# A recurrent head stage with 64-token pair products, its outputs and k^T v in the pair products' PSUM banks, and a planner that counts shape changes

## The chip, the cores and the metric

The kernel runs on one core of one Trainium2 chip. The core has a matrix engine (TensorE, PE in the profile, with PEld for its weight loads), a vector engine (VectorE, DVE), an activation engine (ScalarE, ACT), a general engine (GpSimd, POOL) and a queue engine for transfers (SyncE, SP). The metric is the device time of one execution in microseconds. Before the change it is 3298.43 us, the median of three runs (3298.05 to 3305.83).

## The reference

Input is x of 2 x 4096 x 256 in fp32. A layer norm modulated by a conditioning vector is followed by two RWKV layers (time mix and channel mix), a residual, a second modulated norm and a feed-forward net whose operands are rounded to FP4 in blocks of 16. The change touches the recurrence in the time mix, four heads of 64 channels each:

```python
def step(state, inp):
    rt, kt, vt, wt = inp
    kv = kt[..., :, None] * vt[..., None, :]
    out = jnp.einsum('bhk,bhkv->bhv', rt, state + u[None, :, :, None] * kv)
    return (state * wt[..., None] + kv, out)
```

So the output at a token is r times the decayed sum of all earlier k^T v, with the weight u instead of a decay for the token itself. Each head's output is then scaled to unit variance over its 64 channels.

## The kernel before

**Tiles and streams.** Work goes in tiles of 256 tokens (`TT`), two chunks of 128 tokens (`C`) each. The 256 channels are two groups of 128 (`J`), and each holds two heads of 64 (`HS`). There are 16 tiles per batch element, two batch elements and two layers, so 64 calls of `wkv`. Four generators (`first_layer` and `second_layer`, for each batch element) make the layers' work, a fifth (`ffns`) the feed-forward net of the 32 finished tiles, and two more prepare weights and conditioning.

**The planner.** Every operation is recorded (`record`, `weight` gives its cost) and issued in an order that `Plan.run` chooses: the operation that can start first by the planner's own clock, and among those of its engine that can start within 40 ns (`SOON`) the most urgent, then the oldest. Successive matmuls of a generator make one operation. The clock is not measured, so an operation's place is fixed when the kernel is built. `need` finds dependencies by comparing partitions and columns of a tile. All instructions are issued from one line, line 248 in the profile (`give_out`), so the profile is read by tile names. Evacuated PSUM results live in 36 working tiles (`slot`). Five PSUM banks are shared and handed out at issue (`bank`, `close`).

**The head stage (`wkv`).** A lock (`head_lock`) lets one head stage at a time use `pa`, two PSUM banks, one for each head of a channel group. A stage is more urgent than other work (`RUSH`) while it holds the lock. It runs seven levels. At level l, products of k and r give the scores of token pairs whose positions first differ in bit l, while the decays between them are multiplied into r and k on DVE from level to level (`pair_view`), and the decay products are halved in number. Levels 0 to 4 multiply 32 tokens by 32: per level 2 chunks, 2 groups, 4 blocks and 2 heads, 32 products of 64 channels. Level 5 makes 16 such products off the diagonal, level 6 eight of 64 by 64 tokens. Levels 0 to 3 have a place each in `pa`. After level 3 four masked copies (`copy_predicated`, a mask for each level) collect them in `diag`; level 4 is collected after level 6, when two more plain copies move levels 5 and 6 into `attn`. Four copies then spread `diag` along the diagonal of `attn`.

**Outputs and state.** For each chunk, r is multiplied with the state `S` (128 x 128 for a channel group, two heads, with zeros off the diagonal), the scores in `attn` with v, both into one shared bank `po`; then k^T v of the chunk goes to a bank of its own, `kv`. DVE updates the state from `kv`, ACT squares the outputs, DVE sums the squares. After the second chunk the lock is given back; a power on POOL and one multiplication on DVE scale the outputs from `po` to a working tile.

Of the kernel before, what the change touches and what calls it, by code (L numbers as in the profile page):

```python
# [10 lines left out]
I32 = mybir.dt.int32  # L11
# [20 lines left out]
LEAST = (8, 5, 3)  # L32
RUSH = 1.0
SOON = 40.0
SLOTS = 36
STAGGER = (12, 60)
SLOTS2 = 4
TINY = 24
# [51 lines left out]


class Op:
    __slots__ = ("eng", "calls", "cost", "port", "wait", "ready", "next", "end", "banks", "tiles", "age", "late")

    def __init__(self, eng, age):
        self.eng, self.age = eng, age
        self.calls, self.banks, self.tiles, self.next = [], {}, set(), []
        self.cost = self.ready = self.end = 0.0
        self.port = False
        self.wait = 0  # L100


class Plan:
# [15 lines left out]
    SEEN = {"tensor": 55.0, "gpsimd": 80.0}  # L119
    SAME = {"vector": 34.0, "scalar": 25.0, "gpsimd": 80.0}  # L120

    def after(self, o, op):
        return o.end + (self.SAME.get(o.eng, 0.0) if o.eng == op.eng else self.LAT[o.eng] + self.SEEN.get(op.eng, 35.0))

    def __init__(self, nc, banks):
        self.nc, self.banks = nc, [(0.0, b) for b in banks]
        self.probe = banks[0]
        self.seen = {}
        self.held = {}
        self.free = {e: 0.0 for e in self.ENG}  # L130
        self.lock = {"vector": 0.0, "gpsimd": 0.0}
        self.cur = None
        self.count = 0
        for e in self.ENG:
            setattr(self, e, Recorder(self, e))
# [67 lines left out]
    def record(self, eng, fn, a, k):  # L203
        st = self.cur
        outs = [k["out"]] if "out" in k else [a[0]]
        ins = list(a[0 if "out" in k else 1:]) + [v for n, v in k.items() if n != "out"]
        ins = [v for v in ins if isinstance(v, (bass.AP, Later))]
        cost, port = weight(eng, fn, outs[0], ins)
        op = st.last if eng == "tensor" else None
        if op is None or op.next is None:  # L210
            self.count += 1
            op = Op(eng, self.count)
            op.late = st.late
            st.queue.append(op)
        st.last = op if eng == "tensor" else None
        op.calls.append((getattr(getattr(self.nc, eng), fn), a, k))
        op.cost += cost
        op.port = op.port or port
        for v in ins:
            if not is_dram(v):  # L220
                self.need(op, v, False)
        for v in outs:
            if not is_dram(v):
                self.need(op, v, True)

    def start(self, op, st):
# [7 lines left out]
            t = max(t, self.lock["gpsimd" if op.eng == "vector" else "vector"] - 100.0)  # L234
        return t

    def give_out(self, op, t):
        for b in op.banks:
            if b.real is None:
# [6 lines left out]

        for fn, a, k in op.calls:
            fn(*[real(v) for v in a], **{n: real(v) for n, v in k.items()})  # L248
        op.end = t + op.cost
        self.free[op.eng] = t + (60.0 if op.eng == "sync" else op.cost - self.LAP.get(op.eng, 0.0))  # L250
        if op.port:
            self.lock[op.eng] = op.end
        for b in op.banks:
# [62 lines left out]
        return lambda *a, **k: self.plan.record(self.eng, fn, a, k)  # L316


def is_dram(v):
    return isinstance(v, bass.AP) and v.name.endswith("_dram")  # L320


def weight(eng, fn, out, ins):
# [4 lines left out]

    n = max(v.free_size() for v in [out] + ins)
    if eng == "tensor":  # L330
        if fn == "transpose":
            return 110.0, False
        n = out.free_size()
        if n <= 32:
            return 19.0, False
        pair = (n == 64 and out.shape[0] == 64) or (ins[0].shape[0] <= 64 and out.shape[0] == P and n == TT)
        return (4 * n / 2.4 + 6) * (0.55 if pair else 1.0), False
    if eng == "sync":
        return 100.0, False
    wide = [v for v in ins if v.free_size() > 1]  # L340
# [17 lines left out]
def rwkv_adaln_fp4_kernel(ctx: ExitStack, tc: tile.TileContext, a: dict, out: bass.AP):  # L358
# [28 lines left out]

    masks = const.tile([P, NLEV, 32], I32, name="masks")  # L390
    with tc.tile_pool(name="mk", bufs=1) as mk:
        s_i = mk.tile([P, 32], I32, name="s_i")
        t_i = mk.tile([P, 32], I32, name="t_i")
        x_i = mk.tile([P, 32], I32, name="x_i")
        g_i = mk.tile([P, 32], I32, name="g_i")
        y_i = mk.tile([P, 32], I32, name="y_i")
        nc.gpsimd.iota(s_i, pattern=[[0, 32]], base=0, channel_multiplier=1)
        nc.gpsimd.iota(t_i, pattern=[[1, 32]], base=0, channel_multiplier=0)
        nc.vector.tensor_scalar(s_i, s_i, 31, None, ALU.bitwise_and)
# [9 lines left out]

    ps = ctx.enter_context(tc.tile_pool(name="ps", bufs=1, space=PSUM))  # L410
    pa = ps.tile([P, 2, 512], F32, name="pa")
    kv = ps.tile([P, C, J, P], F32, name="kv")
    banks = [ps.tile([P, 512], F32, name=f"bank{n}") for n in range(5)]

    wk = ctx.enter_context(tc.tile_pool(name="work", bufs=1))

# [165 lines left out]
        pl.comes(t, when)  # L582


    state = [[keep.tile([P, J, P], F32, name=f"S{i}_{b}") for b in range(B)] for i in range(L)]
    carry = [
        [[keep.tile([P, J, 1], F32, name=f"carry{i}_{b}_{m}") for m in range(2)] for b in range(B)]
        for i in range(L)
# [6 lines left out]
    diag = keep.tile([P, 2, C, J, 32], F32, name="diag")  # L595
    attn = keep.tile([P, 2, C, J, P], F32, name="attn")
    nc.gpsimd.memset(diag, 0.0)
    nc.vector.memset(kv, 0.0)
    nc.gpsimd.memset(attn, 0.0)


# [140 lines left out]
    def wkv(i, b, rk_s, dec_s, v_s):  # L742
# [20 lines left out]
        for l in range(7):  # L763
            h = 1 << l
            R, K = (r0, k0) if l == 0 else (r, k)
            wid = 64 if l == 6 else 32
            col0 = (l % 4) * C * J * 32
            cols = slice(col0, col0 + C * J * wid)
            pv = pa[:, :, cols].rearrange("p a (c j t) -> p a c j t", c=C, j=J)

            if l < NLEV:
                at0 = [(q, q) for q in (0, 32, 64, 96)]
            else:
                at0 = [(0, 32), (64, 96)] if l == 5 else [(0, 64)]
            for c in range(C):
# [21 lines left out]
            pl.vector.tensor_tensor(nt, tv[:, :, 0], tv[:, :, 1], ALU.mult)  # L797
            tot = nt

            ready = {3: range(0, 4), 6: range(4, 7)}.get(l, ())  # L800
            for m in ready:
                mw = 64 if m == 6 else 32
                c0 = (m % 4) * C * J * 32
                mc = slice(c0, c0 + C * J * mw)
                if m < NLEV:
                    pl.vector.copy_predicated(
                        diag.rearrange("p a c j t -> p a (c j) t"),
                        masks[:, m, :].unsqueeze(1).unsqueeze(1).to_broadcast([P, 2, C * J, 32]),
                        pa[:, :, mc].rearrange("p a (n t) -> p a n t", t=32),
                    )  # L810
                else:
                    for s0, t0 in [(0, 32), (64, 96)] if m == 5 else [(0, 64)]:
                        pl.scalar.copy(
                            attn[s0 : s0 + mw].rearrange("p a c j t -> p a (c j) t")[:, :, :, t0 : t0 + mw],
                            pa[s0 : s0 + mw, :, mc].rearrange("p a (n t) -> p a n t", t=mw),
                        )
            yield
        give(dec_s)
        tot = tot.rearrange("p (c j) -> p c j", c=C)
        for q in range(4):  # L820
            qs = slice(32 * q, 32 * (q + 1))
            pl.scalar.copy(
                attn[qs].rearrange("p a c j t -> p (a c j) t")[:, :, qs],
                diag[qs].rearrange("p a c j t -> p (a c j) t"),
# [8 lines left out]
        pl.close(bk)  # L833
        yield
        o_s, sq_s = take_slot(), take_slot()
        o_sb, sq = v3(o_s), v3(sq_s)
        bk, po = pl.bank()
        po = halves(po)
        n = C * H
        few = pl.take(tiny)  # L840
        rs = few[:, :n]
        for c in range(C):
            for j in range(J):
                mm(po[:, c, j * P : (j + 1) * P], r[:, c, j, :], S[:, j, :], True, False)
                for p in range(2):
                    hd = slice((2 * j + p) * HS, (2 * j + p + 1) * HS)
                    mm(po[:, c, hd], attn[:, p, c, j, :], v[:, c, hd], False, p == 1)

# [8 lines left out]
            pl.scalar.activation(sq[:, c, :], po[:, c, :], AF.Square)  # L857
# [440 lines left out]
```

## Time and profile before

| | |
|---|---|
| median of three runs | 3298.43 us |
| the profiled execution | 3307.55 us |
| its span in the profile | 3305.8 us |
| mean granted TensorE clock | 0.967 of full speed |
| DMA | 42.31 MB, mean 13 GB/s |
| pair products of 32 tokens (`pa`, 64x32) | 22528 records, mean 200 to 202 ns |
| r times S (`bank<-S,slot`) | 512 records, mean 297 ns |
| attn times v (`bank<-slot,attn`) | 1024 records, mean 264 ns |
| k^T v (`kv`) | 1024 records, mean 235 ns |
| state update on DVE | 256, mean 343 ns |
| activation table loads on ACT | 133, mean 1283 ns |

Durations come from one profiled execution. A row of a group gives its line, engine, operation, output and input names with shapes, the count, the busy time in us and the mean in ns of one, and then the idle time of the engine just before them and what ended it. In a timeline a row gives start, length, engine, group and the number of records. One fp32 matmul is two records. A matmul's record is its whole passage through the array, so records overlap, and the distance from start to start says what it costs; the shape behind the name (64*32) is the rows and columns of the array that it uses.

### The profile page before, as it was taken

Reading aid. Unit: us, or ns where it says so; the run is one execution under the profiler, and the core shown is the slowest. Engines: PE = TensorE matmul, PEld = TensorE weight load, DVE = VectorE, ACT = ScalarE, POOL = GpSimd, SP = SyncE. Lnnn points to the kernel's source line nnn. Section 1 sums busy time; section 2 is a strip of 40 time slices with the busy share of each in tenths; the row PEclk is TensorE's granted clock in tenths of the full one; section 3 lists DMA queues with packets and bytes.
Section 4 is the critical chain, followed back from the end, with each engine's and each line's share of the span. In section 5 each row is a group of like instructions: output and inputs, shape, how many; then the busy total and the mean of one; then the engine's idle time right before and its main releaser. Section 6 shows DMA issues by size and latency. Waiting matters only on the chain. (4 is left out here: it accounts for less than half of the span.)

```text
span 3305.8 us, 88142 instructions
## 1 busy us (share of the span) xinstructions
PE 3075.7 (93%) x37948; PEld 2448.4 (74%) x37948; DVE 2396.8 (73%) x6146; ACT 1628.8 (49%) x3240; POOL 938.5 (28%) x857
## 2 busy tenths in 40 slices
PE   3899999999999999999999999999999999999965
PEld 1678778777777877777887777877777877877743
DVE  3777687777777687777777777778767787866764
ACT  1455455555555555555555555455554555444321
POOL 1233223233223233323233322333322233321200
PEclk8899999999999999999999999999999999998977
DMA  4000000000000000000000000000000000000000
GB/s 126 17 16 5 11 9 14 5 8 14 8 11 5 15 8 11 8 9 11 8 15 8 11 8 5 17 5 15 4 8 15 8 15 8 5 8 8 14 4 10
DMA packets 46856, 42.31 MB, mean 13 GB/s; under 512 B 13185, under 2 KB 44930, under 8 KB 46466
## 3 DMA queue, kind: packets, MB, share of 16 engines
q1 hardware_dynamic: 36962, 31.75, 3.2%
q8 instruction: 298, 4.88, 0.6%
q10 hardware_dynamic: 9504, 4.93, 0.5%
q14 instruction: 92, 0.75, 0.1%
HBM read 28.28 MB, written 8.39 MB: 11 GB/s over the span
## 5 line engine op out<-in xcount | busy, mean ns | idle before, releaser
L248 POOL TENSOR_TENSOR slot<-slot,slot 128x512 f32<-128x512 f32 x416 | 499.5, 1214 | 1016.4 <-DVE slot L248 614.9
L248 ACT ACTIVATE slot<-bank 128x512 f32<-128x512 f32 (+1 forms) x644 | 338.9, 531 | 753.3 <-PE bank L248 714.9
L248 POOL TENSOR_TENSOR tiny<-tiny,nhalf 128x2 f32<-128x2 f32 (+1 forms) x288 | 295.0, 1028 | 1018.2 <-DVE tiny L248 960.5
L248 DVE TENSOR_TENSOR slot<-slot,slot 128x512 f32<-128x512 f32 x512 | 381.6, 747 | 121.4 <-PE pa L248 88.7
L248 PE MATMUL bank<-slot,cWk 128*128 128x256 f32 x1536 | 375.8, 391 | 14.5 <-DVE slot L248 12.3
L248 PE MATMUL bank<-cWv,slot 128*128 128x256 f32 x1536 | 345.4, 381 | 0.0
L248 PEld LDWEIGHTS pa<-slot 64*32 64x32 f32 x19456 | 226.0, 109 | 156.3 <-DVE slot L248 56.5
L248 PEld LDWEIGHTS bank<-slot,cWk 128*128 128x128 f32 x1536 | 289.4, 194 | 62.1 <-DVE slot L248 15.7
L248 PEld LDWEIGHTS bank<-cWv,slot 128*128 128x128 f32 x1536 | 289.4, 190 | 41.0 <-ACT slot L248 0.7
L248 ACT ACTIVATE slot<-bank,vec 128x256 f32<-128x256 f32 x512 | 234.4, 496 | 166.6 <-PE bank L248 159.4
L248 PE MATMUL pa<-slot 64*32 64x32 f32 x19456 | 271.6, 203 | 38.0 <-DVE slot L248 24.0
L248 DVE SCALAR_TENSOR_TENSOR slot<-bank,vec,slot 128x256 f32<-128x256 f32 x640 | 275.1, 474 | 29.5 <-PE bank L248 28.1
L248 DVE TENSOR_TENSOR slot<-slot,bank 128x512 f32<-128x512 f32 x192 | 131.3, 684 | 200.8 <-PE bank L248 173.1
L248 POOL TENSOR_TENSOR slot<-slot 128x512 f32<-128x512 f32 x128 | 143.2, 1120 | 322.8 <-ACT slot L248 253.0
L248 DVE TENSOR_TENSOR long<-long,bank 128x352 f32<-128x352 f32 x256 | 131.7, 515 | 113.9 <-ACT long L248 91.7
L248 ACT ACTIVATE slot<-slot,tiny 128x256 f32<-128x256 f32 x256 | 141.8, 593 | 135.7 <-DVE tiny L248 114.7
L248 PE MATMUL bank<-ident,slot 128*128 128x128 f32 x1152 | 181.3, 286 | 23.9 <-ACT slot L248 18.1
L248 ACT ACT_TABLE_LOAD x133 | 170.6, 1283 | 46.6 <-DMA td<-in_L_attn_td_w_dram 38.3
L248 PE MATMUL bank<-wd,long 128*128 128x256 f32 x768 | 192.3, 403 | 1.2 <-ACT long L248 1.2
L248 PE MATMUL bank<-wg,slot 128*128 128x352 f32 x512 | 180.0, 474 | 4.6 <-ACT slot L248 4.4
L248 PEld LDWEIGHTS bank<-ident,slot 128*128 128x128 f32 x1152 | 136.6, 144 | 61.7 <-ACT slot L248 24.0
L248 DVE SCALAR_TENSOR_TENSOR slot<-slot,vec,slot 128x256 f32<-128x256 f32 x384 | 177.6, 493 | 5.8 <-POOL slot L248 5.7
(112 smaller groups left out, 5837.0 us busy)
## 6 DMA issues: line engine op xcount, KB each, us to landing
slot<-in_L_attn_x_dram SPq DMA_DIRECT2D x63, 256.0 KB, 2.7
out_dram<-slot SPq DMA_DIRECT2D x32, 256.0 KB, 2.1
cWv<-in_L_attn_cWv_dram SPq DMA_DIRECT2D x1, 768.0 KB, 9.4
cWk<-in_L_attn_cWk_dram ACTq DMA_DIRECT2D x1, 768.0 KB, 8.1
slot<-in_L_wmod_dram SPq DMA_DIRECT2D x3, 256.0 KB, 7.3
slot<-in_L_wmod_dram ACTq DMA_DIRECT2D x3, 256.0 KB, 6.5
cWk<-in_L_attn_cWk_dram SPq DMA_DIRECT2D x1, 768.0 KB, 4.8
cWv<-in_L_attn_cWv_dram ACTq DMA_DIRECT2D x1, 768.0 KB, 8.4
```

Of the source, the lines that this page charges most:

```text
L248: fn(*[real(v) for v in a], **{n: real(v) for n, v in k.items()})
```

## The change

1. Levels 0 to 4 multiply 64 tokens by 64: two blocks for the two halves of a chunk, so 16 products per level. `diag` and the masks are 64 tokens wide. A level needs twice the room in `pa`, so there are two places, used in turn. Levels are collected after level 1 (0 and 1), after level 3 (2 and 3), after level 5 (4 and 5) and after level 6. Level 5 goes to `diag`, and two copies of 64 partitions spread `diag` into `attn`.
2. k^T v of both chunks is computed ahead of the outputs, into the first half of `pa`'s first bank.
3. The state holds 64 columns for a channel group instead of 128. r is multiplied with it head by head, 64 channels each, 64 rows of the array at a time: four products of 64 columns per chunk where there were two of 128.
4. The outputs go to the second half of `pa`'s two banks, a bank for each head of a group. The scaling reads them there, and the lock is given back and the urgency ends behind it.
5. `kv` has no bank of its own, and the shared banks are six. There are 35 working tiles.
6. The planner adds a cost where an engine's operation differs in form from its last one: 94 ns on TensorE for another shape, 1283 ns on ScalarE for another of Sigmoid and Exp. Costs of matmuls go by shape.

```diff
-SLOTS = 36
+SLOTS = 35
...
+    TURN = {"tensor": 94.0, "scalar": 1283.0}
...
+        f = form(eng, fn, outs[0], ins, a)
+        if f is not None:
+            if op.forms and op.forms[-1] != f:
+                op.cost += self.TURN[eng]
+            op.forms.append(f)
...
+    def turn(self, op):
+
+        return self.TURN[op.eng] if op.forms and op.forms[0] != self.form[op.eng] else 0.0
...
-        op.end = t + op.cost
-        self.free[op.eng] = t + (60.0 if op.eng == "sync" else op.cost - self.LAP.get(op.eng, 0.0))
+        op.end = t + op.cost + self.turn(op)
+        if op.forms:
+            self.form[op.eng] = op.forms[-1]
+        self.free[op.eng] = t + (60.0 if op.eng == "sync" else op.end - t - self.LAP.get(op.eng, 0.0))
...
+def form(eng, fn, out, ins, a):
+    if eng == "tensor":
+        return (ins[0].shape[0], P if fn == "transpose" else out.shape[0])
+    if eng == "scalar" and fn == "activation" and a[2] in (AF.Sigmoid, AF.Exp):
+        return a[2]
...
-        n = out.free_size()
-        if n <= 32:
-            return 19.0, False
-        pair = (n == 64 and out.shape[0] == 64) or (ins[0].shape[0] <= 64 and out.shape[0] == P and n == TT)
-        return (4 * n / 2.4 + 6) * (0.55 if pair else 1.0), False
+        if rows == P and cols == P:
+            return max(4 * n / 2.4 + 6, 195.0 if n == 64 else 265.0 if n == P else 0.0), False
+        if n <= 64:
+            return {(64, 32): 22.0, (64, 64): 66.0, (P, 64): 70.0, (64, P): 66.0}.get((rows, cols), 2 * n), False
+        return 0.55 * (4 * n / 2.4 + 6), False
...
-    kv = ps.tile([P, C, J, P], F32, name="kv")
-    banks = [ps.tile([P, 512], F32, name=f"bank{n}") for n in range(5)]
+    banks = [ps.tile([P, 512], F32, name=f"bank{n}") for n in range(6)]
...
-    state = [[keep.tile([P, J, P], F32, name=f"S{i}_{b}") for b in range(B)] for i in range(L)]
+    state = [[keep.tile([P, J, HS], F32, name=f"S{i}_{b}") for b in range(B)] for i in range(L)]
...
-            wid = 64 if l == 6 else 32
-            col0 = (l % 4) * C * J * 32
+            wid = 32 if l == 5 else 64
+            col0 = 0 if l == 6 else (l % 2) * C * J * 64
...
-                at0 = [(q, q) for q in (0, 32, 64, 96)]
+                at0 = [(0, 0), (64, 64)]
...
-            ready = {3: range(0, 4), 6: range(4, 7)}.get(l, ())
-            for m in ready:
+            for m in {1: (0, 1), 3: (2, 3), 5: (4, 5), 6: (6,)}.get(l, ()):
...
-        for q in range(4):
-            qs = slice(32 * q, 32 * (q + 1))
+        for q in range(2):
+            qs = slice(64 * q, 64 * (q + 1))
...
-        bk, po = pl.bank()
-        po = halves(po)
+        po = pa[:, :, 256:].rearrange("p a (c j v) -> p a c j v", c=C, j=J)
+        kv = pa[:, 0, :256].rearrange("p (c j v) -> p c j v", c=C, j=J)
...
-                mm(po[:, c, j * P : (j + 1) * P], r[:, c, j, :], S[:, j, :], True, False)
                 for p in range(2):
                     hd = slice((2 * j + p) * HS, (2 * j + p + 1) * HS)
-                    mm(po[:, c, hd], attn[:, p, c, j, :], v[:, c, hd], False, p == 1)
-
+                    mm(kv[p * HS : (p + 1) * HS, c, j, :], kt[:, c, hd], v[:, c, hd], True, True)
+        yield
+        for c in range(C):
+            for j in range(J):
+                for p in range(2):
+                    hp = slice(p * HS, (p + 1) * HS)
+                    mm(po[:, p, c, j, :], r[hp, c, j, :], S[hp, j, :], j == 0, False)
             for j in range(J):
                 for p in range(2):
                     hd = slice((2 * j + p) * HS, (2 * j + p + 1) * HS)
-                    mm(kv[p * HS : (p + 1) * HS, c, j, p * HS : (p + 1) * HS], kt[:, c, hd], v[:, c, hd], True, True)
+                    mm(po[:, p, c, j, :], attn[:, p, c, j, :], v[:, c, hd], False, j == J - 1)
...
-                head_lock.clear()
-                pl.cur.late = late
...
-            o_sb.rearrange("p c (h v) -> p (c h) v", v=HS), po.rearrange("p c (h v) -> p (c h) v", v=HS),
-            rs.unsqueeze(2).to_broadcast([P, n, HS]), ALU.mult,
+            o_s[:, : J * TT].rearrange("p (n a v) -> p a n v", a=2, v=HS),
+            pa[:, :, 256:].rearrange("p a (n v) -> p a n v", v=HS),
+            rs.rearrange("p (n a) -> p a n", a=2).unsqueeze(3).to_broadcast([P, 2, C * J, HS]), ALU.mult,
         )
-        pl.close(bk)
+        head_lock.clear()
+        pl.cur.late = late
```

More of the change, by code (lines that the diff above doesn't have):

```diff
@@ L92 @@
 class Op:
-    __slots__ = ("eng", "calls", "cost", "port", "wait", "ready", "next", "end", "banks", "tiles", "age", "late")
+    __slots__ = ("eng", "calls", "cost", "port", "wait", "ready", "next", "end", "banks", "tiles", "age", "late", "forms")
     def __init__(self, eng, age):
@@ L98, in __init__ @@
         self.cost = self.ready = self.end = 0.0
+        self.forms = []
         self.port = False
@@ L131, in __init__ @@
         self.lock = {"vector": 0.0, "gpsimd": 0.0}
+        self.form = {"tensor": None, "scalar": None}
         self.cur = None
@@ L330, in weight @@
     if eng == "tensor":
+        n, rows, cols = out.free_size(), ins[0].shape[0], out.shape[0]
         if fn == "transpose":
             return 110.0, False
-        n = out.free_size()
-        if n <= 32:
-            return 19.0, False
-        pair = (n == 64 and out.shape[0] == 64) or (ins[0].shape[0] <= 64 and out.shape[0] == P and n == TT)
-        return (4 * n / 2.4 + 6) * (0.55 if pair else 1.0), False
+        if rows == P and cols == P:
[3 more added lines that the diff above has]
+        return 0.55 * (4 * n / 2.4 + 6), False
     if eng == "sync":
@@ L386, in rwkv_adaln_fp4_kernel @@
     nc.gpsimd.memset(nhalf, -0.5)
-    masks = const.tile([P, NLEV, 32], I32, name="masks")
+    masks = const.tile([P, NLEV, 64], I32, name="masks")
     with tc.tile_pool(name="mk", bufs=1) as mk:
[L392 to L399, printed above, removed]
+        s_i = mk.tile([P, 64], I32, name="s_i")
+        t_i = mk.tile([P, 64], I32, name="t_i")
+        x_i = mk.tile([P, 64], I32, name="x_i")
+        g_i = mk.tile([P, 64], I32, name="g_i")
+        y_i = mk.tile([P, 64], I32, name="y_i")
+        nc.gpsimd.iota(s_i, pattern=[[0, 64]], base=0, channel_multiplier=1)
+        nc.gpsimd.iota(t_i, pattern=[[1, 64]], base=0, channel_multiplier=0)
+        nc.vector.tensor_scalar(s_i, s_i, 63, None, ALU.bitwise_and)
         nc.vector.tensor_tensor(x_i, s_i, t_i, ALU.bitwise_xor)
@@ L594, in rwkv_adaln_fp4_kernel @@
                 nc.gpsimd.memset(carry[i][b][m], 0.0)
-    diag = keep.tile([P, 2, C, J, 32], F32, name="diag")
+    diag = keep.tile([P, 2, C, J, 64], F32, name="diag")
     attn = keep.tile([P, 2, C, J, P], F32, name="attn")
     nc.gpsimd.memset(diag, 0.0)
-    nc.vector.memset(kv, 0.0)
     nc.gpsimd.memset(attn, 0.0)
@@ L798, in wkv @@
             tot = nt
-            ready = {3: range(0, 4), 6: range(4, 7)}.get(l, ())
-            for m in ready:
-                mw = 64 if m == 6 else 32
-                c0 = (m % 4) * C * J * 32
+            for m in {1: (0, 1), 3: (2, 3), 5: (4, 5), 6: (6,)}.get(l, ()):
+                mw = 32 if m == 5 else 64
+                c0 = 0 if m == 6 else (m % 2) * C * J * 64
                 mc = slice(c0, c0 + C * J * mw)
@@ L807, in wkv @@
                         diag.rearrange("p a c j t -> p a (c j) t"),
-                        masks[:, m, :].unsqueeze(1).unsqueeze(1).to_broadcast([P, 2, C * J, 32]),
-                        pa[:, :, mc].rearrange("p a (n t) -> p a n t", t=32),
-                    )
-                else:
-                    for s0, t0 in [(0, 32), (64, 96)] if m == 5 else [(0, 64)]:
+                        masks[:, m, :].unsqueeze(1).unsqueeze(1).to_broadcast([P, 2, C * J, 64]),
+                        pa[:, :, mc].rearrange("p a (n t) -> p a n t", t=64),
+                    )
+                else:
+                    dst = diag if m == 5 else attn
+                    for s0, t0 in [(0, 32), (64, 32)] if m == 5 else [(0, 64)]:
                         pl.scalar.copy(
-                            attn[s0 : s0 + mw].rearrange("p a c j t -> p a (c j) t")[:, :, :, t0 : t0 + mw],
+                            dst[s0 : s0 + mw].rearrange("p a c j t -> p a (c j) t")[:, :, :, t0 : t0 + mw],
                             pa[s0 : s0 + mw, :, mc].rearrange("p a (n t) -> p a n t", t=mw),
@@ L835, in wkv @@
         o_s, sq_s = take_slot(), take_slot()
-        o_sb, sq = v3(o_s), v3(sq_s)
-        bk, po = pl.bank()
-        po = halves(po)
+        sq = v3(sq_s)
+        po = pa[:, :, 256:].rearrange("p a (c j v) -> p a c j v", c=C, j=J)
+        kv = pa[:, 0, :256].rearrange("p (c j v) -> p c j v", c=C, j=J)
         n = C * H
@@ L856, in wkv @@
                 )
-            pl.scalar.activation(sq[:, c, :], po[:, c, :], AF.Square)
+            pl.scalar.activation(
+                sq[:, c, :].rearrange("p (j a v) -> p a j v", j=J, a=2), po[:, :, c, :, :], AF.Square
+            )
             pl.vector.tensor_reduce(
```

## The prediction

> **What bounds the kernel now.** First the busy times of the page, then the stages.
>
> ```profile
> span 3305.8 us, 88142 instructions
> PE 3075.7 (93%) x37948; PEld 2448.4 (74%) x37948; DVE 2396.8 (73%) x6146; ACT 1628.8 (49%) x3240; POOL 938.5 (28%) x857
> ```
>
> The matrix engine (PE) is the bound, the vector engine is 20 points behind. The view by windows (columns: window, length, then PE, PEld, DVE, ACT, POOL busy) says where:
>
> ```profile
> 1500.00:2000.00 500.00, 487.17 (x6046) 390.30 (x6047) 377.14 (x966) 265.09 (x524) 155.44 (x140) 1.00 0.04 11
> 3200.00:3306.00 106.00, 60.70 (x193) 42.54 (x191) 53.65 (x100) 16.71 (x31) 5.55 (x5) 0.76 0.02 8
> ```
>
> From 500 to 3000 us PE is busy 97% of the time. The last 180 us are a chain of feed-forward tiles, one output every 38 us, which the change doesn't touch. So the sum is made per head stage (one call of `wkv`, 64 in all, one every 51 us), in PE time. A busy PE hides its gaps, so I take the spacing of starts from PE's timeline (start, length, group, count; one fp32 product is two records):
>
> ```profile
> 2411.03 1.89 PE L248 MATMUL bank<-Wo,slot 128*128 128x256 f32 x8
> 2412.85 0.76 PE L248 MATMUL pa<-slot 64*32 64x32 f32 x64
> 2413.54 0.70 PE L248 MATMUL bank<-slot,w 128*128 128x256 f32 x2
> ...
> 2417.85 0.68 PE L248 MATMUL pa<-slot 64*64 64x64 f32 x16
> 2418.46 0.70 PE L248 MATMUL bank<-slot,w2b 32*128 32x256 f32 x4
> ...
> 2423.07 0.38 PE L248 MATMUL bank<-S,slot 128*128 128x128 f32 x2
> 2423.30 0.56 PE L248 MATMUL bank<-slot,attn 128*128 128x64 f32 x4
> 2423.69 0.44 PE L248 MATMUL bank<-S,slot 128*128 128x128 f32 x2
> 2423.97 0.56 PE L248 MATMUL bank<-slot,attn 128*128 128x64 f32 x4
> 2424.45 0.45 PE L248 MATMUL kv<-slot,slot 128*64 128x64 f32 x8
> 2424.83 1.99 PE L248 MATMUL bank<-Wv,slot 128*128 128x256 f32 x8
> 2426.66 0.38 PE L248 MATMUL bank<-S,slot 128*128 128x128 f32 x2
> ```
>
> To be seen: a level of 32 pair products takes 0.69 us to the next start; level 6 (8 products on two 64x64 tiles) 0.61; one chunk of outputs 1.38, its k^T v 0.38. Eight records of 128x256 are 0.216 each, 1.73, in a row of their own shape; before another shape (Wo) they take 1.82, after one (Wv) 1.83. So leaving a shape costs about 0.10 us and coming back 0.10.
>
> **The change on PE, per head stage.** *Pair levels 0 to 4*: 32 products of 64x32 become 16 of 64x64 on four tiles. No row shows four such tiles. Level 6 ran two row tiles at once (0.61 for 8), k^T v two column tiles at once (0.38 for 4 products), and the present levels eight small ones. If four run at once, 16 products take what 8 take on two, 0.61, with a stagger 0.63; if two at a time, eight more steps of 58 ns (level 6's spacing of record pairs), 1.08. Nearest are the rows that show each split alone: I take 0.63. 5 x (0.63 - 0.69) = -0.30 us; worst +1.95.
>
> *k^T v*: twice 0.38, with 0.10 in and 0.10 out each (1.16; the 0.10 in is inside the 1.38 above), becomes one group of 16 records on two tiles, level 6's 0.61, plus 0.20: 0.81.
>
> *Output products*: the 12 records of a chunk take 1.38, less 0.10 for leaving, 107 ns each, whether 128 or 64 columns stream: what binds is the loading of 128 weight columns. After the change r times S is four products of 64 rows by 128 columns on two row tiles, a shape of its own. Nearest by count is k^T v, 8 records on two tiles in 0.38; but that loads 64 columns. The Trainium skill (TensorE: Matmul & The Clock Gate, LDWEIGHTS) says that a load costs by its columns, not by its rows: 128 columns are 107 ns with 64 rows too. By it the four steps take 4 x 0.11 + 0.05 + 0.10 = 0.60; by the k^T v row 0.38. The 107 ns of the outputs decide for the rule. Then 8 attn records, 8 x 0.11 + 0.10 for re-entry = 0.98, and 0.10 before r times S: 1.68 a chunk. Both chunks with k^T v: 2 x 1.68 + 0.81 = 4.17, against 2 x (1.38 + 0.38 + 0.10) = 3.72 now. +0.45 us: two more shape changes per chunk cost more than the zero blocks.
>
> PE together: -0.30 + 0.45 = +0.15 us x 64 = **+10 us**; ends -18 (r times S at 0.38) and +150 (pairs two at a time).
>
> **DVE and ACT.** The rows by shape:
>
> ```profile
> L248 DVE COPY_PREDICATED diag<-masks,pa 128x256 f32<-128x256 int32 x320 | 139.9, 437 | 23.4 <-ACT attn L248 13.0 <-PE pa L248 7.1 <-ACT slot L248 1.3
> L248 DVE TENSOR_TENSOR long<-long,bank 128x352 f32<-128x352 f32 x256 | 131.7, 515 | 113.9 <-ACT long L248 91.7 <-PE bank L248 20.9
> L248 DVE TENSOR_TENSOR slot<-slot,bank 128x512 f32<-128x512 f32 x192 | 131.3, 684 | 200.8 <-PE bank L248 173.1 <-ACT slot L248 20.4 <-issue 6.1
> L248 ACT COPY attn<-diag 32x256 f32<-32x256 f32 x256 | 103.0, 402 | 17.9 <-DVE diag L248 14.2 <-DVE tiny L248 0.5
> L248 ACT COPY attn<-pa 64x512 f32<-64x512 f32 x64 | 36.6, 572 | 6.8 <-DVE diag L248 6.4
> ```
>
> An element costs (684 - 515) / 160 = 1.06 ns, so the masked copy of 512 columns takes 437 + 256 x 1.06 = 707 ns: 5 x 270 = +1.35 us. Four state updates lose 64 columns (TENSOR_TENSOR of 128 columns 302, of 64 241): -0.24. DVE +1.1 us, 71 us in all, busy from 73% to 75%. ACT: four copies of 402 become two of 572, -0.46. Neither binds; both lie under PE's other work, except in the head's own chain.
>
> **The chain and the shared banks.** Now levels 0 to 3 have four places and are copied together after level 3; only level 4 waits for copies. Its start follows level 3's by 5.2 us in the median, where levels 2, 3 and 5 follow by 2.6 to 3.2. After the change there are two places, and levels 2, 4 and 6 wait for copies of 0.7 us. The planner compares columns (`need`), so it lets one copy run beside the next level. The Trainium skill (PSUM — Partial Sum Buffer, PSUM bank collisions) says that two engines must be kept off one bank and 32-partition quadrant at any columns. The trace agrees: of 512 reads of the pair banks (320 masked, 192 plain) none overlaps a matmul into them. By the planner's rule a level waits for one copy; by the banks', for all that are issued before it, 0.7 us later than planned, and queued behind it in PE's order is everything else. Likewise k^T v and both outputs now lie in these two banks: state updates (DVE), squares (ACT) and the next chunk go one after the other. Cost: nothing if PE arrives late anyway, up to 4 x 0.4 = 1.6 us a stage if it doesn't. The nearest row is level 4: PE lost 3.1 us before it in 64 stages, 0.05 each. Three levels more and the chunks at twice that: 0.25 us x 64 = **+16 us**.
>
> The lock on the pair banks is held longer. From the first pair product to the last k^T v are 31 us in the mean; now the next head may start its pairs earlier, and in 22 of 64 cases did before or within 5 us of that end. After, the banks come free with the scaling, 4 us later at best (9 in the mean, but its urgency now lasts till there), and copies add 1 to 2 us: 36 to 38 us of 51. PE's gaps beyond the spacing of its shape sum to 107 us in the 1650 us inside these stretches and 23 in 850 outside (500 to 3000): 6.5% and 2.7%. Six us longer x 3.8% x 64 = +15; in part it is the above: **+12 us**; ends 0 and +90.
>
> **Planner and sixth bank.** The waits of the weight queue, same window (us, times, longest):
>
> ```profile
> PEld pa L248 <- DVE slot L248: 44.5, 95, 1.5
> PEld bank L248 <- ACT slot L248: 26.9, 50, 2.1
> PEld pa L248 <- ACT slot L248: 18.5, 43, 2.1
> ```
>
> With the smaller rows ACT releases a third of the waits for data, a third of 130 us, 43. The 133 table loads of 1.28 us aren't in today's plan and are in the new one; so are 94 ns for a PE shape, of the 0.20 that it costs. Against this, 64x64 is planned at 66 ns a product where my 0.63 gives 33. Banks: a group holds one about 2.7 us (from a projection's start to its evacuation's end), some 31 groups a stage, plus the output's 15: 2 of 5 in use on average, so a sixth is rarely the one missing. Between 0 and -65 (half of the gaps); I take a third of ACT's share, **-15 us**. One working tile fewer (35 of 36): nothing.
>
> **Sum.** 10 + 16 + 12 - 15 = +23 us. The profiled execution took 3307.55 (span 3305.8, 1.75 around it), 0.3% above the median 3298.43; on the median, **3321 us**.
>
> **Rivals.** *A better plan wins* (not slower): the place is PE's gaps behind ACT and DVE, 130 us. It decides from 38 us removed, the 23 and the 15 already counted. For it: those gaps are waits that a truer plan fills; against: inside a head they come from a chain that gets longer. At half, 65 us: 3298 + 38 - 65 = 3271. *Nothing measurable*: the terms cancel, 3298. *The pair banks become the bound*: 38 us of 51 is no limit for heads spread evenly, but their starts lie 20 to 81 us apart; where two or three streams stand at the lock, PE has one stream and the feed-forward left. At the upper end, +90: 3298 + 11 + 90 = 3399. For it: spacings under 36 us now become impossible; against: long gaps exist into which they can move. *The four tiles don't run together*: (1.08 - 0.63) x 5 x 64 = +144, 3465; against it stand both two-tile rows.
>
> **Chances.** Forecast (3309 to 3365) 0.42; better plan 0.25; nothing 0.13; banks bound 0.15; tiles 0.05. About 0.3% (10 us) is what this kernel's runs can tell from no change. Faster 0.25, same 0.13, slower 0.42 + 0.15 + 0.05 = 0.62. For 8 in 10 the range reaches half into the better plan and most of the way to the banks' case: 3245 to 3400.
>
> **What would show it.** In PE's timeline: 16 products of 64x64 with the next start 0.63 us on (1.08: tiles); r times S at 0.60 (0.38: the load rule wrong); k^T v at 0.61. The masked copy at 707 ns. PE gaps above 130 us between 500 and 3000, with "PE pa <- DVE" grown; from first pair to scaling under 40 us. Wrong if ACT-released waits fall to half, or if heads start at intervals of 40 us in an unbroken row, which is the lock. The tail alone can move it 14 us: one feed-forward tile more or less left at 3130 us (38 us, some 24 of them PE).

## The result and the profile after

The changed kernel takes 3308.68 us (median of 13 runs, 3302.11 to 3323.3) against 3298.71 us: 1.0044 of the time before, with a 95% interval of 1.0026 to 1.0063. It is slower, by 10 us between the medians and by 14 us by the ratio. Two of the 13 executions of before, of 5975 and 11991 us, lie far outside all others and don't enter the ratio. The forecast was 3321 us, its range 3245 to 3400.

The profiled execution took 3320.43 us, span 3318.3, some 12 us above the median, as that of before lay 9 above its own. The page's first lines after the change:

```profile
span 3318.3 us, 68391 instructions
PE 3066.0 (92%) x28220; PEld 2407.3 (73%) x28220; DVE 2490.9 (75%) x6145; ACT 1591.1 (48%) x3112; POOL 947.9 (29%) x857
```

PE's busy time fell by 10 us while the span grew by 12.5, so PE stood idle 22 us longer. Where, the windows show, first of before, then of after (columns: window, length, PE, PEld, DVE, ACT and POOL busy with counts, PE's granted clock, DMA share, GB/s):

```profile
500.00:3000.00 2500.00, 2433.32 (x30748) 1950.23 (x30747) 1866.61 (x4796) 1313.50 (x2602) 753.33 (x670) 0.99 0.03 10
3000.00:3306.00 306.00, 225.28 (x1632) 169.77 (x1631) 190.50 (x417) 87.24 (x170) 45.08 (x40) 0.84 0.03 9
```

```profile
500.00:3000.00 2500.00, 2392.17 (x22360) 1884.99 (x22359) 1922.36 (x4739) 1253.66 (x2444) 752.07 (x658) 0.99 0.03 9
3000.00:3318.00 318.00, 261.95 (x1825) 201.00 (x1823) 212.50 (x476) 112.23 (x216) 55.15 (x49) 0.90 0.03 9
```

In the main stretch PE is idle 108 us instead of 67; behind 3000 us it is idle 56 instead of 81. The head stages end later and the feed-forward net has caught up more by then, so the last stretch is better filled (its granted clock is 0.90 instead of 0.84): the last head stage ends at 3192 us instead of 3125, yet the kernel ends only 12.5 us later.

The products themselves are to be read from PE's timeline (start, length, group, records, and idle time ahead of it with its releaser; all instructions now come from line 262):

```profile
1519.78 0.69 PE L262 MATMUL pa<-slot 64*64 64x64 f32 x32
1520.40 0.70 PE L262 MATMUL bank<-slot,w2b 32*128 32x256 f32 x4
1521.03 0.66 PE L262 MATMUL bank<-ident,slot 128*128 128x128 f32 x4
1522.02 0.69 PE L262 MATMUL pa<-slot 64*64 64x64 f32 x32 [0.34 <-DVE slot L262]
...
1540.91 0.66 PE L262 MATMUL pa<-S,slot 64*128 64x64 f32 x8
1541.50 1.10 PE L262 MATMUL pa<-slot,attn 128*128 128x64 f32 x8
1542.54 0.69 PE L262 MATMUL pa<-slot,slot 128*64 128x64 f32 x16
1543.15 2.86 PE L262 MATMUL bank<-wd,long 128*128 128x256 f32 x12
```

A level of 16 products takes 0.62 us to the next start (0.63 was forecast, 0.69 before), r times S of a chunk 0.59 (0.60), k^T v of both chunks 0.61 (0.61). The state update and the masked copy:

```profile
L262 DVE COPY_PREDICATED diag<-masks,pa 128x512 f32<-128x512 int32 x320 | 231.1, 722 | 8.9 <-PE pa L262 7.3
L262 DVE SCALAR_TENSOR_TENSOR S<-S,slot,pa 128x64 f32<-128x64 f32 x256 | 62.6, 277 | 92.9 <-PE pa L262 54.7 <-ACT slot L262 37.5
```

And what the weight queue (PEld) waits for from 500 to 3000 us (us, times, longest): the waits of the pair products on DVE.

```profile
PEld pa L262 <- DVE slot L262: 63.0, 95, 3.2
...
PEld pa L262 <- DVE diag L262: 31.8, 36, 1.8
```

`DVE slot`, the decayed r and k, was 44.5 before; `DVE diag`, the masked copies, was 3.2. What ACT releases (`slot`, `diag`, `attn` and `long`) is 57 us before and after.

The same from PE's side: its idle time just before the pair products, over the whole span, with what ended it. Before, these are levels 1 to 5; after, levels 1 to 4 and 6:

```profile
L248 PE MATMUL pa<-slot 64*32 64x32 f32 x18432 | 226.7, 202 | 32.5 <-DVE slot L248 21.7 <-DVE diag L248 5.6 <-DVE carry L248 2.5
```

```profile
L262 PE MATMUL pa<-slot 64*64 64x64 f32 x9216 | 222.5, 225 | 61.7 <-DVE diag L262 24.4 <-DVE slot L262 20.4 <-DVE tiny L262 7.9
```

With the level that stands in a row of its own (5.5 us before, 12.0 after) that is 38.0 us before and 73.7 after.

**How gaps and work are told apart below.** I sum what lies between the starts of neighbouring PE records beyond the usual distance of the same pair of shapes; that is "gaps", over the whole span. The span less the gaps is PE's "work", shape changes and reloads included. Before: gaps 295 us, work 3011. After: gaps 293, work 3025. So by this count PE got 14 us more work, the gaps between 100 and 3000 us grew from 170 to 200 us, and those behind 3000 shrank from 110 to 78. Where the line between the two lies depends on what is called usual. A second count from the same records takes blocks of one shape against the usual length of such a block: it finds 3014 us of work before and 3015 after, gaps of 166 and 209 us between 100 and 3000 us, and 109 and 78 behind. The 44 us that the stretch up to 3000 us lost are the same in both (14 + 30, or 1 + 43); a difference of some 15 us in work is not to be relied on.

Gaps before the pair products of levels 2 to 6 are listed apart, since they can be placed: 10.5 us before, 53.9 after. This too is a count of that kind. PE's plain idle time at these places is 11 and 55 us from 500 to 3000 us, and 28 and 70 us over all 64 head stages.

### The profile page after: what moved, and what is told of

The parts are those of the page before. It is cut to its first block, busy times and chain, and to the rows that moved or that the text cites. A ratio compares the mean times of both kernels' runs of the same rounds, so it can differ in the third digit from the quotient of the medians.

```text
span 3318.3 us, 68391 instructions
## 1 busy us (share of the span) xinstructions
PE 3066.0 (92%) x28220; PEld 2407.3 (73%) x28220; DVE 2490.9 (75%) x6145; ACT 1591.1 (48%) x3112; POOL 947.9 (29%) x857
## 5 line engine op out<-in xcount | busy, mean ns | idle before, releaser
L262 POOL TENSOR_TENSOR slot<-slot,slot 128x512 f32<-128x512 f32 x416 | 511.4, 1245 | 892.9 <-DVE slot L262 535.7
L262 ACT ACTIVATE slot<-bank 128x512 f32<-128x512 f32 (+1 forms) x516 | 292.0, 567 | 568.8 <-PE bank L262 551.7
L262 PEld LDWEIGHTS pa<-slot 64*64 64x64 f32 x11264 | 203.7, 132 | 190.1 <-DVE slot L262 72.2
L262 PE MATMUL pa<-slot 64*64 64x64 f32 x11264 | 252.4, 220 | 73.7 <-DVE slot L262 31.6
L262 DVE COPY_PREDICATED diag<-masks,pa 128x512 f32<-128x512 int32 x320 | 231.1, 722 | 8.9 <-PE pa L262 7.3
L262 ACT ACT_TABLE_LOAD x133 | 170.6, 1283 | 48.9 <-DMA td<-in_L_attn_td_w_dram 38.6
```

## The experiments

The ratios are to the kernel before on the same chip. Each profile gives work and gaps.

**A plan that differs for no reason.** 36 working tiles instead of 35:

```diff
-SLOTS = 35
+SLOTS = 36
```

> The changed kernel with 36 working tiles instead of 35: a part of the change undone that should be worth nothing of itself. It shows how far a different but equivalent plan moves the time. Every theory: 3309 us, within 8 us; anything beyond is the chance of the plan, and other differences must be read against it.

Measured 3313.11 us, ratio 1.0047 (1.0029 to 1.0065): the same as the change, as expected; how far another plan can go, one such pair doesn't say. Work 3027, gaps 284; before levels 2 to 6, 45 us.

**The planner of before in the changed kernel** (no forms, no `turn`, the old costs):

```diff
...
-        op.end = t + op.cost + self.turn(op)
+        op.end = t + op.cost
...
```

> The changed kernel with the planner of before (no form changes, old costs); nothing else differs. My theory (the plan is worth 15 us): 3324. Rival (the new plan does harm, since it plans a 64x64 product at 66 ns where 33 are measured): 3295. If within 8 us of 3309, the planner's part is worth nothing.

Measured 3308.11 us, 1.0041 (1.0026 to 1.0056). In this pair of plans the planner's part is worth nothing measurable: neither the 15 us that I counted for it nor harm from a price of 66 ns for a product that costs half. It does move waits: what ACT releases for the weight queue is 75 us with the planner of before and 57 with the new one, while `DVE slot` and `DVE diag` together are 69 with the old and 95 with the new.

**Five shared banks in the changed kernel:**

```diff
-    banks = [ps.tile([P, 512], F32, name=f"bank{n}") for n in range(6)]
+    banks = [ps.tile([P, 512], F32, name=f"bank{n}") for n in range(5)]
```

> The changed kernel with five shared banks, the sixth left unused. My theory (2 of 5 banks in use on average): 3309 to 3315. Rival (the sixth bank is what pays for the rest): 3330 or more.

Measured 3353.3 us, 1.0182 (1.0151 to 1.0212), 45 us above the change, as the rival expected. In the profiles it is 28 us, all of it gaps (327; work 3019). That speaks against my count, by which a sixth bank is rarely missed. How much of the 45 us is the bank's own, and how much a plan that happens to be worse, one run doesn't say (see the halved interpolations below).

**The wide state, outputs in one shape.** The state with its zero blocks again, outputs in the second pair bank; 34 working tiles; the core of the edit:

```diff
-        po = pa[:, :, 256:].rearrange("p a (c j v) -> p a c j v", c=C, j=J)
+        po = pa[:, 1, :].rearrange("p (c n) -> p c n", c=C)
...
-                    mm(po[:, p, c, j, :], r[hp, c, j, :], S[hp, j, :], j == 0, False)
+                mm(po[:, c, j * P : (j + 1) * P], r[:, c, j, :], S[:, j, :], True, False)
...
+                    pl.vector.scalar_tensor_tensor(
+                        S[hp, j, hp], S[hp, j, hp], tot[hp, c, j : j + 1], kv[hp, c, j, :], ALU.mult, ALU.add
+                    )
```

> The changed kernel with the state 128 columns wide again, zero blocks and all: r times S and attn times v go through the array in one shape, as before, into the second pair bank alone, and k^T v stays alone in the first; 34 working tiles. The state update takes 8 instructions of 64 partitions a stage instead of 4. My theory: a chunk's outputs cost 1.38 us of PE again instead of 1.68, -0.6 us x 64 = -38 us, 3271; some of it is lost to the longer state update (0.55 us a chunk), so 3271 to 3285. Rival (the lock and the pair banks set the time, shape changes of PE don't): 3300 to 3312, with PE's gaps grown by what the products gained.

Measured 3413.22 us, 1.035 (1.033 to 1.0369). The work fell to 2979, by 46 us against the change (27 in the second count): the price of the split outputs, 38 us, lies between. But the gaps rose to 435. Both expectations fell; this version has twice the state updates and one tile fewer, which the next runs take apart.

**The same with the outputs in a shared bank, lock given back earlier**, at 35 and at 34 tiles:

```diff
-        po = pa[:, 1, :].rearrange("p (c n) -> p c n", c=C)
+        bk, po = pl.bank()
+        po = halves(po)
...
             if c == C - 1:
+                head_lock.clear()
+                pl.cur.late = late
```

> As the run with the wide state, but the outputs go to one of the six shared banks, so the lock is given back before the scaling, as in the kernel before; 35 working tiles. If the long lock is what made the wide state slow (3413), 3340 or less. If DVE's eight updates did it, 3390 to 3410. If the lock costs the 12 us of my sum, 3400, less what a shared bank costs that is taken for 15 us a stage.

> The run with the wide state and the outputs in a shared bank (3316), with 34 working tiles instead of 35, to be set beside the wide state with the outputs in the pair bank at 34 tiles (3413). If the short lock is worth the 97 us between them: 3316, within 10. If the tile too few is: 3400.

Measured 3315.86 us, 1.0053 (1.0036 to 1.0069), and with 34 tiles 3326.45, 1.009 (1.0075 to 1.0105). Of what was expected, the cases in which the lock made the wide state slow are met, the second nearly. At the same number of tiles the outputs' place and the lock make 87 us: work is equal (2975 and 2979), gaps 349 against 435. With the short lock the next head starts its pairs before the last one's scaling has ended in 24 of 63 cases, with the long one in none. The 10 us of the tile are within what plans differ by. That the halved updates are the whole cause is ruled out: both versions have them.

**Halved state updates.** The changed kernel, each update in two instructions of 64 partitions:

```diff
-                pl.vector.scalar_tensor_tensor(
-                    S[:, j, :], S[:, j, :], tot[:, c, j : j + 1], kv[:, c, j, :], ALU.mult, ALU.add
-                )
+                for p in range(2):
+                    hp = slice(p * HS, (p + 1) * HS)
+                    pl.vector.scalar_tensor_tensor(
+                        S[hp, j, :], S[hp, j, :], tot[hp, c, j : j + 1], kv[hp, c, j, :], ALU.mult, ALU.add
+                    )
```

> The changed kernel with each state update in two instructions of 64 partitions instead of one of 128: the same result, 256 more DVE instructions of 0.28 us, 71 us of DVE time in all, and nothing else. My theory of the prediction (DVE at 75% is hidden, only the chain from chunk to chunk gets 0.55 us longer): at most 3320. Rival (DVE's time, not PE's, is what PE's gaps come from): the 71 us show nearly whole, 3360 or more, and the run with the wide state, 3413, was slow for that reason.

Measured 3370.61 us, 1.0217 (1.0192 to 1.0242), 62 us above the change (57 by the ratios); work 3028, gaps 341. DVE's busy time rose by 82 us. The rival's number is met; whether for the rival's reason, the next run asks.

**DVE time outside the head stage.** Each interpolation in two halves:

```diff
-            pl.vector.scalar_tensor_tensor(
-                m[:, j, :], sx[:, j, :], maa[:, j : j + 1], x[:, j, :], ALU.mult, ALU.add
-            )
+            for q in (slice(0, P), slice(P, TT)):
+                pl.vector.scalar_tensor_tensor(
+                    m[:, j, q], sx[:, j, q], maa[:, j : j + 1], x[:, j, q], ALU.mult, ALU.add
+                )
```

> The changed kernel with each interpolation of the inputs (lerp, 128x256, 384 of them) in two instructions of half the columns: 384 more instructions, about 85 us of DVE time, all of it outside the stretch in which a head holds the pair banks. If DVE's time as such is what PE's gaps come from, it costs what the halved state updates did for each us: 85 x 62 / 71 = 74 us, 3383. If only DVE time inside the locked chain counts: 3325 or less.

Measured 3264.96 us, 0.9903 (0.9885 to 0.9922): 44 us *faster* than the change and clearly faster than the kernel before, with this row on DVE:

```profile
L262 DVE SCALAR_TENSOR_TENSOR slot<-slot,vec,slot 128x128 f32<-128x128 f32 x768 | 238.0, 358 | 11.0 <-POOL slot L262 11.0
```

That is 54 us of busy time more on this row, 45 on DVE as a whole. Work is unchanged (3028), gaps 242. The second expectation, 3325 or less, is met in the letter, but no theory expected a gain. That DVE's time as such makes PE's gaps is refuted; that DVE's time inside the locked chain does, as in the halved updates, stays possible. Why this plan is better isn't shown: shorter instructions let a head's urgent ones in sooner, but the operations' ages and how far a stream is recorded ahead, which is counted in operations, change as well. What it does show is that a plan can move by some 45 us with no change in PE's work, so a difference of that size between two plans is no evidence by itself. The 45 us of the five banks and the 62 of the halved updates stand under this reservation.

**64-token pairs alone, in the kernel before**: the loop, masks and `diag` of the change and its 35 working tiles, with a larger reserve of tiles (`LEAST`).

```diff
-            wid = 64 if l == 6 else 32
-            col0 = (l % 4) * C * J * 32
+            wid = 32 if l == 5 else 64
+            col0 = 0 if l == 6 else (l % 2) * C * J * 64
...
-LEAST = (8, 5, 3)
+LEAST = (9, 6, 3)
...
```

> The kernel before with the 64-token pair products alone (two places, copies after levels 1, 3, 5 and 6, masks and diag 64 wide); bank for k^T v, output bank, wide state, five banks and the old planner stay. The streams' reserve of working tiles is 9, 6, 3 instead of 8, 5, 3, and the working tiles are 35. My theory: PE -19 us, but levels 2, 4 and 6 wait for copies in their own banks (in the changed kernel PE lost 54 us before levels 2 to 6 against 11 before, +43): 3298 - 19 + 43 = 3322. Rival (PE's work alone counts): 3280.

Measured 3374.12 us, 1.0233 (1.0204 to 1.0262). Work 2989, 22 us less than before (19 forecast); gaps 381, 86 more, of which 32 lie before levels 2 to 6. Both expected numbers are missed, by 50 us and more. A good part of the rest lies before the feed-forward net's transposes (`bank<-ident,long`): between 100 and 3000 us PE is idle there for 45 us instead of 2, nearly all of it until DVE has their input (`long`) ready. Why the net is so late in this plan isn't shown, and the reserve of tiles wasn't tried alone.

**32-token pairs in the changed kernel**, 36 tiles:

```diff
-            wid = 32 if l == 5 else 64
-            col0 = 0 if l == 6 else (l % 2) * C * J * 64
+            wid = 64 if l == 6 else 32
+            col0 = (l % 4) * C * J * 32
...
-            for m in {1: (0, 1), 3: (2, 3), 5: (4, 5), 6: (6,)}.get(l, ()):
+            ready = {3: range(0, 4), 6: range(4, 7)}.get(l, ())
+            for m in ready:
...
```

> The changed kernel with 32-token pair products again (four places, copies after levels 3 and 6, masks and diag 32 wide); k^T v, outputs, state, planner and six banks as changed; 36 working tiles, since 35 leave the planner no order. PE +19 us, DVE -91 us in masked copies. The state updates in halves made 71 us of DVE cost 62. If a us of DVE in the head stage costs that much: 3309 + 19 - 79 = 3249. If DVE is hidden and only the waits before levels 2 to 6 go (54 us to 11): 3309 + 19 - 43 = 3285. If 64-token products pay: 3320 or more.

Measured 3282.66 us, 0.9955 (0.9939 to 0.9972): faster than the kernel before. Against the same kernel with 64-token pairs and 36 tiles (3313.11) it gains 30 us. Work rose by 14 (3041 against 3027), gaps fell by 44 (241 against 284), and of these 32 lie before levels 2 to 6 (13 against 45). The masked copy, PE's idle time before levels 1 to 5 (both over the whole span), and the waits of the pair products from 500 to 3000 us:

```profile
L262 DVE COPY_PREDICATED diag<-masks,pa 128x256 f32<-128x256 int32 x320 | 140.2, 438 | 20.6 <-ACT attn L262 9.2 <-PE pa L262 7.1 <-ACT slot L262 1.4
L262 PE MATMUL pa<-slot 64*32 64x32 f32 x18432 | 226.4, 201 | 25.2 <-DVE diag L262 10.2 <-DVE slot L262 8.0 <-issue 4.5
```

```profile
PEld pa L262 <- DVE slot L262: 26.5, 68, 1.2
...
PEld pa L262 <- DVE diag L262: 9.5, 14, 1.8
```

`DVE slot` is 26.5 instead of 63.0, `DVE diag` 9.5 instead of 31.8 (65.7 and 33.3 in the version with 36 tiles). Here the gain is found where it was looked for: 64-token pairs save PE 14 us and cost it some 32 in waits. Of the numbers expected, 3285 (DVE hidden, only these waits go) is hit.

The 30 us alone are no more than plans can differ by. The place of the waits is firmer: PE's idle time before levels 1 to 6 is 38, 28 and 27 us in the three versions with 32-token pairs (the kernel before, this one and the last one below) and 55 to 101 us in all eleven with 64-token pairs, whatever else they change.

**A planner that knows the banks.** It treats the two pair banks as one region and every access to them as a write; 36 working tiles:

```diff
         p0, p1, lo, hi = self.region(probe)
+        if not isinstance(ap, Later) and key.startswith("pa"):
+            p0, p1, lo, hi, writes = 0, P, 0, 1024, True
```

> The changed kernel whose planner treats the two pair banks as one region, so that it knows that a level waits for every copy issued before it; 36 working tiles. The work is the same. My theory (PE's waits before levels 2 to 6, 54 us, come from a plan that compares columns while the banks serialise): they fall to 15 or so, 3270. Rival (they come from the longer chain and from DVE being late): 3300 to 3313.

Measured 3318.29 us, 1.0062 (1.0041 to 1.0082). The gaps before levels 2 to 6 stay at 44 us. So knowing the banks doesn't take them away: the rival, the longer chain of copies with DVE late in it, is what remains, and 32-token pairs, which shorten that chain, did take them away.

**What the runs speak for, together**: 32-token pairs, outputs in one shape in a shared bank, short lock, a state of 64 columns that ACT copies into the blocks of a wide one.

```diff
...
+        def widen(c):
+            for p in range(2):
+                hp = slice(p * HS, (p + 1) * HS)
+                pl.scalar.copy(wide[hp, c, :, hp], S[hp, :, :])
...
```

> Parts that the runs speak for together: 32-token pair products, planner, six banks and k^T v first as changed; outputs in one shape with a wide state, in a shared bank, lock given back before the scaling; the state itself 64 columns, updated in 4 DVE instructions a stage, and copied to the wide one by ACT, four copies a stage; 36 working tiles. PE -46 + 19 us against the changed kernel (the wide state took 46 us of PE's work away), DVE -91 us, ACT +75 us of copies. If DVE in the head stage counts: 3309 - 27 - 79 = 3203. If PE's work alone counts: 3282. If the shared bank and the copies on ACT eat it: 3300.

Measured 3260.19 us, 0.9888 (0.9873 to 0.9902), the fastest of all. Its outputs on PE and the added copies:

```profile
1523.88 0.49 PE L262 MATMUL bank<-wide,slot 128*128 128x128 f32 x2
1524.20 0.56 PE L262 MATMUL bank<-slot,attn 128*128 128x64 f32 x4
1524.60 0.44 PE L262 MATMUL bank<-wide,slot 128*128 128x128 f32 x2
1524.87 0.56 PE L262 MATMUL bank<-slot,attn 128*128 128x64 f32 x4
1525.27 0.61 PE L262 MATMUL bank<-ident,slot 128*128 128x128 f32 x4
```

```profile
L262 ACT COPY wide<-S 64x128 f32<-64x128 f32 x256 | 75.1, 294 | 43.1 <-DVE S L262 41.2
```

A chunk's outputs take 1.39 us (1523.88 to 1525.27) where the split ones take 1.63 (1540.91 to 1542.54 above) and another shape change. Against the run with 32-token pairs the work fell by 38 us (3003 against 3041), the gaps rose by 11; the 22 us gained are PE's work. 75 us on ACT were hidden. None of the three expected numbers (3203, 3282, 3300) is hit; the low one had counted DVE time as if all of it showed.

## Why the prediction was right, and where its terms were not

The direction was right, and the measured time lies well inside the range: +23 us forecast, +10 measured, with the median (3308.68) at the lower edge of the likeliest case (3309 to 3365). But the sum came out through terms that were off both ways, so that it came so near is in part luck.

- **PE's products** (+10): the whole span gives +14, or 1 in the second count. Each shape was met within 0.02 us, the load rule included: r times S at 0.59, not the 0.38 of the k^T v row. Undoing the parts moved the work about as priced: 22 and 14 us for the pairs (25 and 17 in the second count; 19 forecast), 46 for the split outputs and the extra shape changes (27; 38 forecast).
- **DVE** (masked copy 707 ns, update 282): 722 and 277. DVE's busy time rose by 94 us instead of 71. That it is hidden as such held outside the head stage, where 45 us more of it made nothing slower. Inside it, 82 us more went with 62 us more time.
- **Waits before levels 2 to 6 and between chunks** (+16): the mis-sized term. The gaps before these levels alone grew by 43 us. I took level 4's loss, 0.05 us, for each new wait; with 64 columns and two places it is 0.17 on average over the five levels (53.9 us in 320 cases), or 0.22 as idle time (70 us). The 0.05 rested on little: over all 64 stages PE was idle before level 4 only seven times, 8.1 us in all. Nor are levels 2, 4 and 6, which wait for a place, all of it: as idle time they grew by 28 us, and levels 3 and 5, for which the forecast had nothing, by 13. And the mechanism was named wrongly in part: the planner's comparing by columns isn't the cause, since a planner that sees the banks loses as much. What the runs point to is the chain: level 2 follows level 1 by 4.4 us in the median instead of 3.2, level 6 level 5 by 3.7 instead of 2.4 (level 4 follows level 3 by 4.5 instead of 5.2), and 32-token pairs take these waits away (2.6, 2.3 and 5.1).
- **The longer lock** (+12): the stretch from first pair product to scaling is 37.1 us in the median, as forecast (36 to 38), but before it was 38.9: the scaling, now urgent, ends 4.8 us behind the last product on average instead of 9.4. In the mean, in which the forecast gave its 31 us for the lock before, the stretch is 39.3: the lock is held 8 us longer, not 6. What changed with it is the shortest distance of two heads, 31.4 us instead of 20.3. Its price in this kernel wasn't isolated; in the version with the wide state, lock and outputs' place made 87 us, far more than 12.
- **Planner and sixth bank** (-15): no share of the planner is found. The sixth bank may be worth up to 45, which I had put at nearly nothing; if so, it paid for a part of the waits, but that isn't shown.
- **The tail**, outside the sum ("14 us, one feed-forward tile more or less"): it gave back 32 us of gaps. The stretch up to 3000 us lost 14 + 30 = 44 us, about twice the +23 of the forecast; the better filled end took 32 of these back.

So the rival "a better plan wins" failed at its named place, the planner, though plans as such can be worth as much. "Nothing measurable" missed narrowly. "The pair banks become the bound" didn't come true: the heads start 31 to 91 us apart, in no unbroken row. Nor do they in the wide state with the long lock (34 to 100 us), so the 87 us of that version aren't explained by it. "Tiles don't run together" is refuted by the 0.62 us.

What stays open: why the feed-forward net is late where the pairs alone are changed, what part of the five banks' 45 us is the bank's, and why halved interpolations give a plan 44 us better.

## What to carry to other kernels

On an engine that is 97% busy, price the products from start to start, shape changes included: that sum held to some 10 us in the versions here, while busy times hid it. Then expect the gaps to decide, and test a part by the place of the gaps that it should move, since a list schedule whose work is the same can shift by 45 us. Work that shortens the bound engine but lengthens the serial chain under a lock (wider masked copies, fewer places) can cost more than it saves: here 14 us saved and some 32 lost in waits, and the narrow pairs with everything else kept were the better kernel, by 30 us.

## What the runs showed that was not expected

- Cutting 384 DVE instructions in two, with 45 us more DVE time in all, made the kernel 1.3% faster than the change, at the same work on PE.
- k^T v, recorded ahead of the outputs, runs ahead of them in only 11 of 64 head stages: in the fence above the first chunk's outputs come at 1540.91 and k^T v at 1542.54.
- Zero blocks in a state are cheap. Four products of 64 rows take as long as two of 128 rows with the zeros: each pair of records that runs at once takes 0.11 us, as one record of 128 rows does, while k^T v with weights of 64 columns has 0.06 a pair. So the columns of the weights decide, not the rows, and the two shape changes come on top (0.59 us in all).
